# In the planner that writes the order of each engine, a hop between engines counts ten times what it did

## The chip, the cores and the metric

The kernel runs on one core of a Trainium2 chip. Five engines of that core matter here: PE (matrix multiplies), ACT (activations and copies), DVE (vector operations), POOL (here almost only the issue of gathers from memory) and SP (the issue of plain transfers). Each engine works through its own list of instructions in the order in which they are written, and they meet only through semaphores: an instruction whose data another engine makes waits for that engine's semaphore, and what stands behind it on its own engine waits as well.

The metric is the device time of one execution in microseconds. It is given as the median of three plain executions. Beside it there is one execution under the hardware profiler, which takes longer and from which all durations of single instructions come.

## What is computed

The input is 16 graphs of 1024 nodes with 64 channels, and an adjacency matrix for each graph in float32. Per graph, the reference normalizes the node features and clips them at zero, drops one or two neighbours, chosen by their rank, of every node that has more than ten (in both directions), and then takes, for every node and channel, a weighted sum of the three quartiles over the neighbours that remain and the node itself. A small two-layer perceptron follows, and the input is added:

```
h = relu(layernorm(x))
adj_d = adj without the edges dropped by rank (made symmetric)
s = sort over neighbours of h[neighbour]          # per node, per channel
agg = 0.25*q(0.25) + 0.5*q(0.5) + 0.25*q(0.75)    # quantiles read from s, interpolated
y = relu((h + agg) @ W1 + b1) @ W2 + b2
out = x + y * mask
```

## The kernel before

The fast path (`list_layer`; a dense path stands behind a flag that is not set with these inputs) goes through the 16 graphs as 8 pairs. For each graph there is a preparation and an aggregation.

The preparation of a graph is spread over PE, ACT and DVE. `load` reads the adjacency in eight tiles of 128x1024 (line 870), takes its sign on ACT (958), transposes it on PE (965) and writes it back from PSUM by ACT or DVE (978). `drop` computes the distance of each neighbour's rank from the two ranks that are dropped (PE 1035 and 1040, ACT `dist` 1045) and compares on DVE (`rem` 1046). `keep` puts the kept edges together (PE 1058 to 1063, ACT 1068) and packs them to codes (PE 1071, ACT 1076). `order` sorts the nodes by how many neighbours they have (DVE `num` 1082 onwards, `perm` 1117), and `collect` permutes the codes (PE 1142) and reads the neighbours' numbers out of them with repeated maxima on DVE (1151, 1174). The result is a list of row numbers per graph (`idx`, 1186).

The aggregation of a pair begins with gathers: POOL issues one indirect transfer per neighbour slot and tile of 128 nodes (line 1329, 952 of them, and 34 of kin for a special group of nodes with many neighbours, lines 1681, 1685 and 1749). DVE then runs sorting networks over the gathered lines (minima and maxima, lines 1434 to 1442), ACT or DVE scales the chosen lines (1457, 1459), PE adds them up (1463), and the perceptron follows (1564 to 1660).

The Python code emits all this pair by pair; it then hands the whole list of instructions to `arrange`, which decides in what order each engine executes its own. `arrange` makes a `Step` of each instruction, with an estimate of how long it occupies its engine (`busy`) and how long after that its result can be used (`lag`; 200 for PE, 150 for ACT, 80 for DVE, 950 for a gather after 1345 of issue, 1500 and more for a transfer of SP, all in planned ns). It collects the dependencies, the reuse of buffers among them, and walks over the graph of steps forward and backward: each walk is list scheduling, in which an engine that is free takes, of the steps whose inputs are ready, the one of lowest rank. The backward walk gives the ranks for the next forward walk. Six rounds are made (`ROUNDS`), the sequence with the shortest planned end is kept, and it is written down as the order of each engine with ordering edges.

`between(s, o)` is what a walk adds between the end of step `s` and the start of a dependent step `o`. If they are on different engines, or `s` is a transfer, it is the lag and a constant; on DVE itself it is 115, and on the other engines zero.

Two more things come out of the kept walk. Each gather waits until the last gather but one has been issued (`paced`). And each gather is tied to DVE by a leash: it may not be issued before the DVE step that by the plan had ended 25,000 ns (`LEASH`) ahead of it.

Of the kernel before, what the change touches and what calls it, by code (L numbers as in the profile page):

```python
# [70 lines left out]
GROUP = 8  # L71
SLICE = P // GROUP
SECOND = 14
ROUNDS, LEASH = 6, 25000


TURNED = (0, 1, 3, 2, 0, 1, 3, 2)
# [590 lines left out]

def between(s, o):

    return s.lag + 60 if o.engine != s.engine or s.moves else 115 if s.engine == "DVE" else 0


def forward(steps, ranks):

    left, ready = [len(s.before) + len(s.behind) for s in steps], [0.0] * len(steps)
    starts, sequence, wire = [0.0] * len(steps), {e: [] for e in ENGINES}, [0.0]

    def place(s, when, free_to_go):
        starts[s.place] = when  # L680
        sequence[s.engine].append(s)
        end = when + s.busy
        if s.engine == "SP":
            wire[0] = max(wire[0], end) + s.load
            s.lag = wire[0] + 1500 - end
        for o in s.after:
            ready[o.place] = max(ready[o.place], when if s.place in o.behind else end + between(s, o))
            left[o.place] -= 1
            if not left[o.place]:
                free_to_go(o.place, ready[o.place])  # L690

    total = spread(steps, list(left), ranks, place)
    return sequence, starts, total


def backward(steps, starts):

    left, ready, ends = [len(s.after) for s in steps], [0.0] * len(steps), [0.0] * len(steps)

    def place(s, when, free_to_go):  # L700
        ends[s.place] = when + s.busy
        for p in (*s.before, *s.behind):
            o = steps[p]
            ready[p] = max(ready[p], when + s.busy - o.busy if p in s.behind else when + s.busy + between(o, s))
            left[p] -= 1
            if not left[p]:
                free_to_go(p, ready[p])

    spread(steps, list(left), [-(starts[s.place] + s.busy) for s in steps], place)
    return [-t for t in ends]  # L710
# [99 lines left out]
def list_layer(  # L810
# [682 lines left out]
    def aggregate(m, o, between=None):  # L1493
# [4 lines left out]
        for half in (0, 1) if last else (1, 0):  # L1498
            parts = CLASSES[2 * half:2 * half + 2][::1 if last else -1]
            for sides in ((0, 1), (1, 2)) if last and half else ((0, 2),):  # L1500
# [13 lines left out]
                if one is not None:  # L1514
                    yield from between(one, False)
# [528 lines left out]
```

## Time and profile before

| | |
|---|---|
| median of three plain executions | 1444.05 us |
| lowest and highest of the three | 1441.54 and 1449.81 us |
| the profiled execution's own time | 1901.87 us |
| its span, first to last instruction | 1900.1 us |
| busy in the span: PE, DVE, ACT, POOL | 1228.6, 1226.8, 1069.1, 1027.3 us |
| mean granted clock of PE | 0.809 |

The profiled execution is longer than a plain one by 458 us. A share of busy time is to be read against the span of 1900.1 us of the profiled execution, not against the median. The busy time of PE is modelled and its matrix multiplies overlap, so that it overstates how full PE is. A line of the profile's page gives, for a group of like instructions, the source line, engine, operation, the tiles written and read, the count, the busy time in us with the mean in ns, and after the second bar the idle time of that engine just before them, with what ended most of it.

### The profile page before, as it was taken

What the parts mean: (1) busy time and instruction counts of PE and PEld (TensorE: products, weight loads), DVE (VectorE), ACT (ScalarE), POOL (GpSimd) and SP (SyncE); (2) the same over time, 40 slices, a digit from 0 to 9 for tenths busy, and PEclk for the clock granted to TensorE, in tenths of its full rate; (3) what the DMA queues carried; (4) which work ended last, traced back from release to release, by engine and by line L of the source; (5) the groups of instructions that cost most, each with busy time, mean ns of one, the idle gap of its engine ahead of it and who ended that gap; (6) DMA issues with size and microseconds to landing.
All of it is one profiled execution on the core that took longest, in us unless ns stands there. A gap on an engine that the chain in (4) does not pass through costs nothing. (4 is left out here: it accounts for less than half of the span.)

```text
span 1900.1 us, 30251 instructions
## 1 busy us (share of the span) xinstructions
PE 1228.6 (65%) x8995; PEld 770.5 (41%) x9011; DVE 1226.8 (65%) x5869; ACT 1069.1 (56%) x2869; POOL 1027.3 (54%) x991
## 2 busy tenths in 40 slices
PE   6637566577867587667664687655873678733847
PEld 4424344254444344344432444433542345511434
DVE  5515277653676758774658658586757745596895
ACT  7646356466663578355662657353673675323765
POOL 0354564644564646554557455465565645577780
PEclk9769689597888798878877798767986789866868
DMA  5423232212331214121322123231230110112110
GB/s 185 137 76 92 61 92 67 83 50 68 84 102 43 86 39 137 42 73 45 102 79 50 54 47 104 54 94 32 54 71 18 31 21 20 19 23 49 27 31 15
DMA packets 128832, 121.67 MB, mean 64 GB/s; under 512 B 95730, under 2 KB 96274, under 8 KB 128658
## 3 DMA queue, kind: packets, MB, share of 16 engines
q1 hardware_dynamic: 97106, 87.29, 15.3%
q0 software_dynamic: 31552, 32.36, 8.7%
q8 instruction: 73, 1.20, 0.3%
q14 instruction: 101, 0.83, 0.1%
HBM read 108.79 MB, written 9.05 MB: 62 GB/s over the span
## 5 line engine op out<-in xcount | busy, mean ns | idle before, releaser
L1329 POOL DMA_INDIRECT g<-gtab,idx x952 | 989.4, 1039 | 816.3 <-issue 211.8
L1437 DVE TENSOR_TENSOR g<-g 128x384 f32<-128x384 f32 (+2 forms) x659 | 310.9, 492 | 25.1 <-issue 10.7
L1442 DVE TENSOR_TENSOR g<-g 128x384 f32<-128x384 f32 (+2 forms) x659 | 310.1, 491 | 10.1 <-DMA gg<-g 6.0
L1142 PE MATMUL codeP<-pack,perm 128*128 128x332 bf16 x1024 | 191.7, 332 | 59.2 <-DVE perm L1117 38.3
L1045 ACT ACTIVATE dist<-rk,bias 128x512 f16<-128x512 f32 x256 | 169.2, 701 | 84.5 <-remote 44.2
L1068 ACT ACTIVATE kept<-kp 128x512 fp8e4<-128x512 f32 x224 | 133.4, 600 | 132.9 <-remote 61.1
L978 ACT ACTIVATE ne<-tp 128x512 fp8e4<-128x512 f32 x248 | 143.4, 612 | 102.7 <-remote 67.4
L965 PE MATMUL tp<-kb,sg 128*128 128x128 bf16 x1024 | 119.9, 250 | 98.7 <-issue 37.5
L1463 PE MATMUL acc<-g,kf 128*128 128x128 f32 (+2 forms) x472 | 146.2, 446 | 55.7 <-ACT g L1457 35.5
L1035 PE MATMUL rk<-kb,cnt 128*128 128x512 bf16 x256 | 113.7, 444 | 93.6 <-ACT dist L1045 47.4
L1142 PEld LDWEIGHTS <-perm 128*128 128x128 bf16 x1024 | 100.1, 105 | 151.5 <-DVE perm L1117 49.4
L1040 PEld LDWEIGHTS <-ne 128*128 128x128 fp8e4 x1024 | 91.0, 110 | 154.7 <-issue 131.1
L1046 DVE TENSOR_SCALAR rem<-dist,half 128x1024 bf16<-128x1024 f16 x128 | 62.9, 493 | 129.4 <-ACT dist L1045 120.0
L965 PEld LDWEIGHTS <-sg 128*128 128x128 bf16 x1024 | 89.2, 113 | 140.8 <-issue 119.6
L1071 PE MATMUL code<-kw,kept 128*128 128x17 fp8e5 x1024 | 66.2, 175 | 122.4 <-ACT kept L1068 74.5
L958 ACT ACTIVATE sg<-at 128x1024 bf16<-128x1024 f32 x122 | 130.6, 1070 | 4.8 <-DMA at<-in_adj_dram 4.7
L1457 ACT ACTIVATE g<-g,coef 128x64 f32<-128x64 f32 x336 | 87.8, 339 | 79.0 <-DVE g L1437 44.1
L1058 PE MATMUL kp<-ne,kw 128*128 128x512 fp8e4 x256 | 112.7, 441 | 23.0 <-ACT cnt L1007 8.4
L1071 PEld LDWEIGHTS <-kept 128*128 128x128 fp8e4 x1024 | 54.1, 102 | 175.8 <-ACT kept L1068 98.6
L856 DVE MEMSET pause<- 128x1 bf16 x2043 | 120.5, 59 | 2.3 <-issue 2.3
L1463 PEld LDWEIGHTS acc<-g,kf 128*128 128x128 f32 x472 | 87.5, 224 | 84.0 <-ACT g L1457 43.1
L1040 PE MATMUL rk<-kw,ne 128*128 128x128 fp8e5 x1024 | 120.5, 245 | 0.0
(202 smaller groups left out, 2489.2 us busy)
## 6 DMA issues: line engine op xcount, KB each, us to landing
at<-in_adj_dram SPq DMA_DIRECT2D x122, 512.0 KB
g<-gtab,idx POOLq DMA_INDIRECT x952
xt<-in_x_dram SPq DMA_DIRECT2D x16, 256.0 KB
y<-in_x_dram SPq DMA_DIRECT2D x16, 256.0 KB
gtab<-xt SPq DMA_DIRECT2D x16, 256.0 KB
out_dram<-y SPq DMA_DIRECT2D x14, 256.0 KB
spare<-in_adj_dram SPq DMA_DIRECT2D x6, 512.0 KB
gg<-g SPq DMA_DIRECT2D x32, 48.0 KB
```

Of the source, the lines that this page charges most:

```text
L856: tails[nc.vector.memset(pause[:, at:at + 1], 0.0).ins.name] = ins.ins.name
L958: nc.scalar.activation(sg, at, AF.Sign)
L965: run.append(nc.tensor.matmul(tp[:, s], sg[:, m * P:(m + 1) * P], ident16, start=(s == 0), stop=(s == 3 and t // 4 != n), skip_group_check ...
L978: nc.scalar.activation(to, tp, AF.Relu, saturate=False)
L1040: run.append(nc.tensor.matmul(rk[:, s * P:(s + 1) * P], ne[:, 4 * n + s, ts], upper, start=False, stop=(s == 3), skip_group_check=True,))
L1045: nc.scalar.activation(dist[:, n * HALF:(n + 1) * HALF], rk, AF.Abs, bias=bias[:, t:t + 1])
L1068: nc.scalar.activation(kept[:, 4 * n:4 * n + 4], kp, AF.Relu, saturate=False)
L1142: run.append(nc.tensor.matmul(flat, perm[:, t, k * P:(k + 1) * P], pack[:, t], start=False, stop=(t == NT - 1), skip_group_check=True,))
L1329: ins = nc.gpsimd.indirect_dma_start(out=gathered[m, tiles][:, slot, k - lo, h], out_offset=None, in_=tables[2 * m + h][0], in_offset=bass ...
L1437: nc.vector.tensor_tensor(at(f + k * df, df, many), pa, pb, OP.min if what == "<" else OP.max)
L1442: nc.vector.tensor_tensor(pa if back else pb, pa, pb, OP.max if what == "<" else OP.min)
L1463: nc.tensor.matmul(acc, ident32, lines[:, s], start=False, stop=(s == now[-1] and not ends), skip_group_check=True)
```

## The change

One constant is added, and the planner's hop from one engine to another (or from a transfer to its user) becomes the lag and 600 instead of the lag and 60. No instruction, tile, buffer or constant of cost is touched beside it; ranks, order, and the places at which the leash is tied follow from the walks.

```diff
-ROUNDS, LEASH = 6, 25000
+ROUNDS, LEASH, LATE = 6, 25000, 600
...
 def between(s, o):

-    return s.lag + 60 if o.engine != s.engine or s.moves else 115 if s.engine == "DVE" else 0
+    return s.lag + LATE if o.engine != s.engine or s.moves else 115 if s.engine == "DVE" else 0
```

## The prediction

> **What bounds the kernel now.** I read the page's totals first, then POOL's gathers in order of time, the waits, the end of the chain, and the busy time by stretch.
>
> From the page, totals and two groups:
>
> ```profile
> span 1900.1 us, 30251 instructions
> PE 1228.6 (65%) x8995; PEld 770.5 (41%) x9011; DVE 1226.8 (65%) x5869; ACT 1069.1 (56%) x2869; POOL 1027.3 (54%) x991
> ...
> L1329 POOL DMA_INDIRECT g<-gtab,idx x952 | 989.4, 1039 | 816.3 <-issue 211.8
> ...
> L1046 DVE TENSOR_SCALAR rem<-dist,half 128x1024 bf16<-128x1024 f16 x128 | 62.9, 493 | 129.4 <-ACT dist L1045 120.0
> ```
>
> No engine is full. POOL looks emptiest, but its shown durations are not its pace. POOL in order of time (start, duration, idle before):
>
> ```profile
> 63.14 1.10 POOL L1329 DMA_INDIRECT g<-gtab,idx  x1 [61.24 <-DVE idx L1186]
> 64.54 0.95 POOL L1329 DMA_INDIRECT g<-gtab,idx  x1 [0.30 <-issue]
> 65.80 0.94 POOL L1329 DMA_INDIRECT g<-gtab,idx  x1 [0.30 <-DMA g<-gtab,idx]
> ...
> 1676.30 1.13 POOL L1329 DMA_INDIRECT g<-gtab,idx  x1 [0.30 <-DMA g<-gtab,idx]
> 1677.73 1.13 POOL L1329 DMA_INDIRECT g<-gtab,idx  x1 [0.30 <-DMA g<-gtab,idx]
> ...
> 1854.87 0.93 POOL L1749 DMA_INDIRECT out_dram<-gx,gto  x1 [1.46 <-DMA out_dram<-gx,gto]
> ```
>
> Back to back, 0.30 us always stays between two gathers: the pace is 1.25 us when quiet and 1.43 us when busy. POOL's 991 instructions are 986 transfers and 5 small ones at the start (1.4 us busy). So POOL occupied is 1025.9 + 986 x 0.30 = 1321.7 us. The head before the first gather is 63.1 us, the tail after the last transfer 1900.1 - 1855.8 = 44.3 us. 63.1 + 1321.7 + 44.3 = 1429.1; POOL waited for the other 471.0 us of the span.
>
> The waits (us in total, times, longest):
>
> ```profile
> POOL g L1329 <- issue: 211.8, 446, 14.1
> DVE rem L1046 <- ACT dist L1045: 120.0, 43, 19.0
> DVE num L1082 <- ACT pack L1076: 88.5, 11, 17.3
> ACT st L1155 <- DVE keys L1151: 82.8, 28, 22.2
> PE code L1071 <- ACT kept L1068: 74.5, 43, 8.5
> POOL g L1329 <- DVE g L1442: 69.4, 47, 12.7
> ```
>
> PE, ACT and DVE wait in turn for each other, and POOL for DVE, mostly by the leash. By gather number POOL's waits are even: some 415 of the 471 us fall before the 800th.
>
> The plain run. The profiled execution (1901.87) is 457.8 us above the median of 1444.05, which is almost what POOL waits. If head and tail are in a plain run what they are here, 1444 - 1429 = 15 us of waiting are left there; if they shrink like the whole (factor 0.759, 107.4 to 81.5), 41 us. **So in a plain run POOL is nearly the bound: about 28 us of idle time, with DVE (1226.8 of 1444 us, 85%) close behind.**
>
> **What the skill says.** Trainium skill, "Perfetto Trace Analysis", "GPSIMD Engine Instruction": a span there is unreliable, and starts of consecutive instructions should be compared. The trace agrees: 0.95 us shown, 1.25 us apart. The same page, "Tensor Engine Instruction (MATMUL, LD_WEIGHTS)": ACT, DVE and GPSIMD are strict FIFO. The trace agrees: `rem` held DVE for up to 19.0 us. "DMA: Bandwidth & Descriptors", "Anatomy of one DMA": a fixed cost of about 2.0 us, mostly completion; the chain below has 2.47 us for a gather. The first walk counts 1345 + 950 + 60 = 2355 ns, the new one 2895.
>
> **The change, part by part.** Instructions, transfers and buffers are the same on every engine; the price of what is removed or added is nothing. Only places change.
>
> The real hop, from the chain that ended last:
>
> ```profile
> 1569.22 2.47 DMA g<-gtab,idx
> ...
> 1762.23 0.59 ACT highs L1621
> 1762.87 2.07 PE hp L1627 x2
> ```
>
> PE starts 0.05 us after ACT's recorded end. The planner's old 210 (ACT) to 260 ns (PE), counted from the engine's release, are near that; 750 to 800 are too long. The plan is thus no truer, it has more room.
>
> (1) Room between producer and user. I took both built orders, and for each wait on another engine summed the mean durations (profile's rows) of the instructions of the waiting engine that stand between the user and the last instruction of its own that must precede the awaited one. Medians, before and after: PE waiting for ACT 3.26 and 4.68 us, ACT for PE 1.90 and 2.60, DVE for PE 2.38 and 3.29, DVE for ACT 4.68 and 5.52. ACT's waits for PE with under 2 us of room fall from 575 to 356. PE's rows overlap, so only the comparison counts. The waits among PE, ACT and DVE shown above are those whose room grows.
>
> (2) POOL's demands. By order and waits together, the 300th gather needs 375 us of DVE work finished before, 313 after; the 600th 766 and 694; the 800th 1021 and 978; the 900th 1129 and 1094. For 43 to 72 us DVE may be later than now without POOL noticing, 35 to 54 gathers at 1.34 us. I count two thirds of the waits before gather 800 as gone: 415/471 x 28 = 25 us, two thirds are 16 us. From below: none, if the waits that remain in plain runs are of the late part; from above all 41.
>
> (3) Head. Ahead of the first gather stand 70 ACT instructions in place of 83 (49 us of rows for 55, ACT being 48.35 of 63 us busy there), 833 of PE for 887, 125 of DVE for 130. But SP's first two transfers become the constants (222 and 144 KB), and the adjacency tile that starts ACT comes third; in the trace ACT starts on it at 4.29 us. At the 178 GB/s of that stretch 366 KB are 2 us. Together 6 - 2 = 4 us earlier; bounds -8 and +4. By the 20th gather 82 us of ACT are needed for 74, by the 50th 107 for 109: the gain is given back there, and I count 0.
>
> (4) Tail. After the 980th gather hang 30 us of DVE for 19, 28 of ACT for 22, 48 of PE for 42. Part lies beside each other: +3 us; bounds 0 and 11. The last two fetches of `gx` (L1685) move to POOL's end, next to the scatter; two places, no new transfer. SP's other moves (28 places at most) are transfers issued tiles ahead; POOL's gather order is the same for 750 of 996 places: 0.
>
> Sum: -16 + 0 + 3 = -13 us of the plain run. On the profiled execution the waits are larger (471 us), and it should fall by more, some 50 to 120 us. Since (2) could as well be the whole 25, I take -16: **1428 us**.
>
> **The rivals.**
> - *Gathers already saturated* (chance 0.21). In favour: the 15 us end above. Then the order is not felt: 1444, within 7.
> - *Late backlog, slower* (0.20). The work taken from before the gathers is still to be done: behind gather 800, DVE has 250 us where it had 178 (1271 us in all). 186 gathers at 1.34 are 249 us, so that from there on DVE must be nearly full, in the stretch where it runs the long sorts:
>
> ```profile
> core 0: us, PE busy (x) PEld busy (x) DVE busy (x) ACT busy (x) POOL busy (x), PEclk, DMA share, GB/s
> 1600.00:1700.00 100.00, 56.50 (x431) 43.98 (x430) 68.08 (x295) 38.94 (x125) 62.01 (x59) 0.80 0.11 20
> 1700.00:1800.00 100.00, 54.84 (x251) 30.56 (x251) 72.18 (x329) 49.17 (x123) 71.94 (x62) 0.74 0.18 39
> 1800.00:1900.00 100.00, 59.20 (x292) 38.60 (x293) 75.58 (x198) 61.33 (x177) 45.04 (x31) 0.76 0.11 22
> ```
>
> Mean share 0.72. With the plain head of 48 us gather 800 is due at 48 + 800 x 1.34 = 1120; 250/0.72 = 347 gives 1467. It decides when the share is under 250/(1444 - 1120) = 0.77. Against it: this execution is stretched; scaled by 85/65 the share is 0.94, and 1120 + 266 = 1386 doesn't bind.
> - *Large gain* (0.07). If plain gathers keep the quiet pace, 986 x 1.25 = 1233, and waits in plain runs are 1444 - 1233 - 82 = 129; a third gone gives about 1400. Against: the busy stretches show 1.43.
> - *No effect on the order* (0): all five orders differ; DVE's instructions move by 30 places in the median, 754 at most.
>
> **How the numbers follow.** The forecast has 0.52. Likeliest 1428, its own range 1408 to 1438. A difference under 0.5% (7 us) is about what a measurement of this kernel can't tell from none. Nearly all of the forecast's case and the large gain lie beyond it: faster 0.58; same 0.21, slower 0.21. For 8 in 10 the range runs from 1398, so that half the large gain is left out, to 1463, so that the upper part of the backlog is.
>
> **What would show.** Right: in the new profile POOL's idle time at L1329 falls well under 816 us, `rem` waits for `dist` under 120, the head stays near 63 us, and DVE's share after 1600 us rises. Wrong: POOL's idle stays, or moves to the last 200 gathers; the tail exceeds 55 us; or sorts wait for gathers, which would say that a longer plan let POOL fall behind.

## The result, and the profile after

The changed kernel takes 1467.71 us in the median of four executions (1466.74 to 1469.96); the kernel before, in its four of the same comparison, 1445.86 us. The ratio is 1.0155, with a 95% interval of 1.0135 to 1.0175: slower by 22 us, where the forecast was 16 us faster.

The 458 us by which the profiled execution of before lies over the plain ones are not a cost of profiling, as the text ahead of the prediction has it. In e1_base, the same kernel, the profiled execution took 1443.97 us, among ten executions from 1441.34 to 1447.28. And on one other chip (the runs e9 to e12) 43 executions of before took 1895.36 to 1928.04 us, with 1901.87 us well inside. So the first profile was most likely taken on such a chip, though its chip is not on record. It can't be laid beside a profile of 1464.9 us; e1_base supplies one of before at 1442.3 us.

The page of the changed kernel, totals and gathers:

```profile
span 1464.9 us, 30188 instructions
PE 1151.5 (79%) x9011; PEld 731.7 (50%) x9011; DVE 1220.3 (83%) x5869; ACT 1047.2 (71%) x2869; POOL 1055.2 (72%) x991
...
L1329 POOL DMA_INDIRECT g<-gtab,idx x952 | 1012.3, 1063 | 357.3 <-DMA g<-gtab,idx 141.3
```

The page of the kernel before, run again (e1_base):

```profile
span 1442.3 us, 30251 instructions
PE 1103.4 (77%) x8995; PEld 709.9 (49%) x9011; DVE 1220.6 (85%) x5869; ACT 1041.3 (72%) x2869; POOL 1046.6 (73%) x991
...
L1329 POOL DMA_INDIRECT g<-gtab,idx x952 | 1005.4, 1056 | 355.3 <-DMA g<-gtab,idx 127.5
```

Of the 355.3 us of idle time before, 952 x 0.30 = 286 us are the fixed distance between gathers and 61.7 us the head; some 8 us are left. In the changed kernel it is 357.3 us, nearly the same. POOL waits for next to nothing in either. What differs is what DVE has done by the time of a given gather. Busy time by stretch, cut at the start of POOL's first, 300th and 900th transfer and at the end; transfers are counted from 0 here and below, so that 86 of the 986 lie behind the last cut. First the kernel before (e1_base):

```profile
core 0: us, PE busy (x) PEld busy (x) DVE busy (x) ACT busy (x) POOL busy (x), PEclk, DMA share, GB/s
63.30:462.90 399.60, 332.34 (x3108) 214.79 (x3109) 333.52 (x1604) 333.35 (x887) 307.50 (x301) 0.97 0.41 116
462.90:1268.60 805.70, 621.07 (x4918) 400.85 (x4926) 713.10 (x3676) 551.12 (x1602) 619.45 (x600) 0.89 0.28 72
1268.60:1442.30 173.70, 105.23 (x517) 64.92 (x521) 135.08 (x455) 108.53 (x294) 118.50 (x86) 0.78 0.15 34
```

and the changed kernel, cut at the same transfers:

```profile
64.40:458.90 394.50, 311.05 (x2675) 199.91 (x2673) 279.98 (x1326) 294.31 (x784) 300.35 (x300) 0.86 0.37 106
458.90:1272.70 813.80, 671.16 (x5247) 423.65 (x5245) 749.73 (x3883) 587.38 (x1674) 629.13 (x601) 0.91 0.29 77
1272.70:1464.90 192.20, 122.96 (x648) 77.42 (x647) 152.10 (x532) 116.71 (x325) 124.59 (x86) 0.78 0.14 31
```

The gathers run at the same pace, but during the first 300 DVE does 280.0 us of work in place of 333.5. In the next 600 it recovers 36.6 us of the 53.5, and 17.0 us more are left behind gather 900. The 22.6 us between the spans are: head 1.1, first 300 gathers -5.1, next 600 +8.1, the rest +18.5. A second profile of the changed kernel on another chip (e15_changed) repeats it: 278.5 us of DVE in the first stretch, and 152.7 in a last stretch of 196.9 us. DVE is not alone: behind gather 900 PE too has 17.7 us more (123.0 for 105.2) and ACT 8.2. DVE is the busiest of the three there, 79% of the stretch for PE's 64%.

Why DVE does less: what it waits for, the kernel before (e1_base) and then the changed one (us in total, times, longest us):

```profile
DVE rem L1046 <- ACT dist L1045: 29.9, 23, 2.8
DVE keys L1151 <- PE codeP L1142: 27.0, 40, 1.2
...
DVE g L1437 <- DMA g<-gtab,idx: 6.1, 3, 3.6
```

```profile
DVE g L1437 <- DMA g<-gtab,idx: 48.7, 16, 10.9
DVE keys L1151 <- PE codeP L1142: 33.0, 34, 2.2
DVE g L1528 <- ACT g L1525: 27.0, 6, 7.5
DVE rem L1046 <- ACT dist L1045: 26.5, 20, 3.5
```

A wait that is small in the kernel before stands first: sorts wait for gathers, 48.7 us for 6.1. The same view for the first stretch of the changed kernel alone (64.4 to 458.9 us) has among others:

```profile
DVE g L1437 <- DMA g<-gtab,idx: 24.9, 7, 10.9
...
DVE g L1528 <- ACT g L1525: 14.0, 3, 7.5
DVE var L1244 <- ACT var L1243: 9.4, 2, 5.9
```

In that stretch DVE is idle for 114.5 us in place of 66.1. Of the 48.4 us more, 24.9 are sorts that wait for gathers (none there before), 13.4 are the step at line 1528, which waits for ACT, 8.6 are `var`, and the rest lies in smaller waits, up and down. In the new order sorting steps come ahead of preparation steps: by the 100th gather DVE has done 35 sorting steps for 23 before, and 93.7 us of preparation (lines below 1230) for 109.1. In the three longest of those waits for gathers (8.4, 3.7 and 10.9 us) the next preparation step stands 4 to 9 instructions behind, and it begins without a wait when its turn comes; that its input was there during the wait is not shown. The wait that the forecast wanted to shrink, `rem` for `dist`, loses 3.4 us.

### The profile page after: what moved, and what is told of

It is laid out like the page before. It is cut to its first block, busy times and chain, and to the rows that moved or that the text cites. A ratio compares the mean times of both kernels' runs of the same rounds, so it can differ in the third digit from the quotient of the medians.

```text
span 1464.9 us, 30188 instructions
## 1 busy us (share of the span) xinstructions
PE 1151.5 (79%) x9011; PEld 731.7 (50%) x9011; DVE 1220.3 (83%) x5869; ACT 1047.2 (71%) x2869; POOL 1055.2 (72%) x991
## 5 line engine op out<-in xcount | busy, mean ns | idle before, releaser
L1329 POOL DMA_INDIRECT g<-gtab,idx x952 | 1012.3, 1063 | 357.3 <-DMA g<-gtab,idx 141.3
L1437 DVE TENSOR_TENSOR g<-g 128x256 f32<-128x256 f32 (+2 forms) x659 | 312.4, 492 | 51.2 <-DMA g<-gtab,idx 48.7
L1442 DVE TENSOR_TENSOR g<-g 128x384 f32<-128x384 f32 (+2 forms) x659 | 310.7, 492 | 3.5 <-DMA gg<-g 2.6
L965 PE MATMUL tp<-kb,sg 128*128 128x128 bf16 x1024 | 113.5, 243 | 56.7 <-ACT dist L1045 28.5
L1142 PEld LDWEIGHTS <-perm 128*128 128x128 bf16 x1024 | 97.5, 102 | 86.0 <-DVE perm L1117 22.9
L1040 PE MATMUL rk<-kw,ne 128*128 128x128 fp8e5 x1024 | 113.9, 239 | 0.0
L1063 PEld LDWEIGHTS <-rem 128*128 128x128 bf16 x1024 | 80.5, 99 | 66.8 <-issue 10.6
L1155 ACT CAST st<-codeP 128x4 bf16<-128x4 f32 x128 | 21.2, 166 | 126.9 <-DVE rest L1153 87.4
L1058 PE MATMUL kp<-ne,kw 128*128 128x512 fp8e4 x256 | 99.4, 390 | 14.6 <-ACT kept L1068 10.0
L1463 PEld LDWEIGHTS acc<-g,kf 128*128 128x128 f32 x472 | 79.5, 212 | 53.0 <-ACT g L1457 23.4
L1059 PE MATMUL kp<-rem,kw 128*128 128x512 bf16 x256 | 99.9, 390 | 2.8 <-DVE pause L856 1.5
```

The lines of the kernel that those rows point to most:

```text
L965: run.append(nc.tensor.matmul(tp[:, s], sg[:, m * P:(m + 1) * P], ident16, start=(s == 0), stop=(s == 3 and t // 4 != n), skip_group_check ...
L1040: run.append(nc.tensor.matmul(rk[:, s * P:(s + 1) * P], ne[:, 4 * n + s, ts], upper, start=False, stop=(s == 3), skip_group_check=True,))
L1142: run.append(nc.tensor.matmul(flat, perm[:, t, k * P:(k + 1) * P], pack[:, t], start=False, stop=(t == NT - 1), skip_group_check=True,))
L1329: ins = nc.gpsimd.indirect_dma_start(out=gathered[m, tiles][:, slot, k - lo, h], out_offset=None, in_=tables[2 * m + h][0], in_offset=bass ...
L1437: nc.vector.tensor_tensor(at(f + k * df, df, many), pa, pb, OP.min if what == "<" else OP.max)
L1442: nc.vector.tensor_tensor(pa if back else pb, pa, pb, OP.max if what == "<" else OP.min)
```

## The experiments

All sixteen run against the kernel before on their own chip; the ratio to that kernel, with its 95% interval, says more than the time. "Held" is the sum, over the last 86 transfers of POOL, of what each shows over 1.4 us, taken from POOL in order of time: what gathers lose by lasting long. The two theories at the start: A, that the loss lies behind gather 900; B, that the gathers' pace falls throughout.

**e1_base: the kernel before again.**

```diff
-ROUNDS, LEASH, LATE = 6, 25000, 600
+ROUNDS, LEASH, LATE = 6, 25000, 60
```

> The kernel before, with the hop of 60 written as the constant. The profile on record of before was stretched to 1900 us; this one should be near its median, 1446 us, so that the two orders can be compared gather by gather. Theory A (the late part): POOL's gathers already keep their pace through the middle here too, at 1.30 to 1.36 us each, with few waits, and the 100th to 900th gather take within 10 us of what they take in the changed kernel (1077 us); what the changed kernel loses lies in the last 86 gathers, which take 154 us there and some 130 us here, and in what is tied to them. Theory B (the whole pace): the gathers run at 1.32 us in the middle here against 1.35 us there, some 20 us over 800 gathers, and the last 86 take the same in both.

Ratio 1.0006. The 100th gather starts at 191.2 us and the 900th at 1268.6: 1077.4 us, and 1077.2 in the changed kernel. B falls. The last 86 take 145.6 us here and 153.8 there, less apart than A had it; the tail after them is 28.1 us and 38.4.

**e2_moves and e3_engines: which hops.** The longer hop for landings alone, then for hops between engines alone (in this cut and the one of e9 and e10, `...` stands for the rest of the line, and the names behind `#` are added here):

```diff
-    return s.lag + LATE if ...
+    return s.lag + (LATE if s.moves else 60) if ...      # e2_moves
+    return s.lag + (60 if s.moves else LATE) if ...      # e3_engines
```

> The change alone for the results of transfers and gathers (lag and 600), while hops between engines keep lag and 60. Theory A: what hurts is where the late gathers and the vector work that uses them are put; if the longer landing makes that, this version is as slow as the changed kernel, 1460 to 1470 us. If the hops between PE, ACT and DVE make it, it stays within 8 us of the kernel before, 1438 to 1454 us. Theory B expects it near the kernel before, since transfers are few and a busier mixture comes from the hops between engines.

> The change alone for hops between engines (lag and 600), while the results of transfers and gathers keep lag and 60. The other half of the run before it: near 1467 us if the hops between PE, ACT and DVE carry the loss, within 8 us of 1446 us if the landings do. Theory B expects 1460 to 1470 us here.

e2_moves: 1438.56 us, ratio 0.9992 (0.9963 to 1.0021). e3_engines: 1461.4 us, 1.0112 (1.0083 to 1.0142). The hops between the engines carry the loss, or most of it. In e3 DVE has 154.6 us left at gather 900, in e2 129.6.

**e4_mid: a hop of 240.**

```diff
-ROUNDS, LEASH, LATE = 6, 25000, 600
+ROUNDS, LEASH, LATE = 6, 25000, 240
```

> The hop counts 240 (four times the old one). If the loss grows with the hop as the plan's length does, some 7 us over the kernel before, 1453 us. If it comes from single places of the order, as theory A has it, the time need not lie between the two; anything from 1430 to 1475 us.

1448.16 us, 1.0023 (1.0006 to 1.004), and 136.4 us of DVE behind gather 900 (135.1 before). Between the two, nearer to the old end, and below the 1453 us of a loss that grows with the hop; the range given for single places was too wide to tell anything.

**e5_rows: the fetches of gx.** At the end of the changed kernel DVE stands for `gx`, whose fetches had moved to POOL's end:

```profile
DVE gx L1660 <- DMA gx<-in_x_dram,gto: 7.7, 1, 7.7
```

The edit, in `arrange`, holds the last pair's gathers into the tiles g6 back behind them:

```diff
+    rows = [s for s in steps if s.engine == "POOL" and any(u.tile.name.startswith("gx") for u in s.writes)][-2:]
+    for s in steps:
+        if s.engine == "POOL" and s.place > rows[-1].place and any(u.tile.name.startswith("g6") for u in s.writes):
+            s.behind.update(o.place for o in rows)
```

> The changed kernel, but the planner is told that the two fetches of gx (L1685) stand ahead of the last pair's g6 gathers on POOL; by the order of the build they then stand at places 950 and 951 of 986, as in the kernel before, and not at 982 and 983. Theory A: at the end of the changed kernel DVE waits 7.7 us for gx (L1660), with the last sorts behind it. That wait goes, the tail after POOL's last transfer falls from 38 us towards 28 to 31, and the time is 1457 to 1461 us. Rival C (the tail is bound by PE's and ACT's own work, and DVE's wait is slack): 1465 to 1469 us.

1471.0 us, 1.0189 (1.0139 to 1.0239): nothing gained. The wait for `gx` is gone, and the waits of sorts for gathers behind gather 900 go from 8.1 to 25.6 us. A's part about `gx` isn't borne out. It isn't a clean test, though, since one gather lasts 13.93 us here and the held time goes from 30.6 to 38.7 us.

**e6_paused, e7_base_paused, e8_both: held gathers.** In the changed kernel two gathers last 12.0 and 6.8 us (POOL in order of time: start, duration, idle before):

```profile
1331.02 1.17 POOL L1329 DMA_INDIRECT g<-gtab,idx  x1 [0.30 <-DVE gg L1442]
1332.50 11.97 POOL L1329 DMA_INDIRECT g<-gtab,idx  x1 [0.30 <-DVE y L1660]
1344.78 6.79 POOL L1329 DMA_INDIRECT g<-gtab,idx  x1 [0.32 <-DVE y L1660]
1351.87 0.94 POOL L1329 DMA_INDIRECT g<-gtab,idx  x1 [0.30 <-DMA g<-gtab,idx]
```

while DVE sorts without a gap, as it does in the last pair and the last group alone, where the 59 ns memset that otherwise follows each sorting step is left off:

```profile
1332.49 0.55 DVE L1442 TENSOR_TENSOR g<-g 128x384 f32<-128x384 f32 x1
1332.96 0.35 DVE L1437 TENSOR_TENSOR gg<-gg 128x192 f32<-128x192 f32 x1
1333.23 0.28 DVE L1434 TENSOR_TENSOR g<-g 128x128 f32<-128x128 f32 x1
```

The Trainium skill, "SBUF — State Buffer", "Who interferes with whom", says that a DVE instruction with two SBUF inputs contends with a GpSimd instruction that reads SBUF; it tells of one instruction, and here a gather is held over a long row of them. The same section infers that `tensor_tensor`, which the sorts are, doesn't stall the issue of transfers; these gathers, long beside rows of it, speak against that. The edit puts the memsets back (e6 in the changed kernel, e7 in the one before, e8 in the changed one with e5's edit too):

```diff
-        gap = (lambda ins: ins) if whole else opened
+        gap = opened
```

> The changed kernel, but the last pair's and the last group's sorts too have the small pause after each vector operation (312 pauses more, 59 ns each, 18 us of DVE). Theory A: single gathers of the changed kernel last 4 to 12 us where DVE sorts without a pause (32.5 us above 1.4 us per gather in all). With pauses no gather lasts over 2.5 us and the last 86 take some 120 us in place of 154; the time falls by 10 to 25 us, to 1443 to 1457. Here the plan also puts the two fetches of gx at 950 and 975, so up to 8 us of a gain may be theirs. Rival D (the long gathers are slack, DVE's work sets the end): 18 us of DVE are added and the time is 1470 to 1485 us.

> The same pauses in the kernel before, where the gathers' excess over 1.4 us is 24.4 us in all. Theory A: 1425 to 1440 us. Rival D: 1450 to 1462 us.

> The changed kernel with both: the fetches of gx at 950 and 951 and the pauses. If both effects are what they seem, the time is that of the kernel before with the pauses, within 8 us. If something else of the changed order costs as well (before gather 900 it is 4 us late), it stays some 5 us or more above it.

e6: 1453.85 us, 1.0061 (1.004 to 1.0083). e7: 1444.57 us, 0.9991 (0.9964 to 1.0019), its executions lying between 1431 and 1448. e8: 1453.51 us, 1.0085 (1.0051 to 1.012). Held time falls from 30.6 us (changed) and 22.9 (before) to 1.7 in e6 and e8 and 0.7 in e7. The stretch from gather 900 to the end, e7 and then e8:

```profile
1271.00:1430.70 159.70, 104.50 (x517) 64.83 (x521) 132.28 (x730) 103.14 (x270) 88.33 (x86) 0.79 0.16 37
```

```profile
1275.80:1454.20 178.40, 119.05 (x643) 75.32 (x647) 153.59 (x836) 115.21 (x318) 94.58 (x86) 0.82 0.15 33
```

The pauses take 14.0 us from this stretch in the kernel before (173.7 to 159.7) and 13.8 in the changed one (192.2 to 178.4, with e5's edit). The difference of 18.5 stays, as 18.7, though hardly a gather is held in either. In these two profiles, then, the held gathers are a cost of both kernels, and what remains is the work left over.

The medians say less. They agree for the changed kernel (14 us less) and not for the kernel before, whose median doesn't move: e7's expectation was met only by its three fastest executions, and its profile is one of these, 12 us under its median. e6 lies inside theory A's 1443 to 1457 us. With the pauses in both kernels the medians are 9 us apart (1453.5 in e8, 1444.6 in e7) and not 22. These 9 us are clear of the noise, as the intervals of e7 and e8 don't meet; whether the other 13 us of the loss go with held gathers or with the luck of single executions stays open. Of e8's two cases it is the second: something else of the changed order costs as well.

The profile of e6 also limits what the pauses do. Its profiled execution took 1467.13 us, 13 us over the median, and has two gathers of 5.26 and 8.99 us ahead of the 900th, among sorts with the memset. This one, in e11_moves_paused below, lasts over 42 memsets:

```profile
1806.98 20.68 POOL L1329 DMA_INDIRECT g<-gtab,idx  x1 [2.59 <-DVE gg L1442]
```

So the memset makes held gathers rarer, and doesn't exclude them.

**e9_early, e10_late, e12_zero, e11_moves_paused.** The longer hop for the first 12,000 of 16,027 steps, or for the others alone; a hop of the lag alone; and the landings' hop with the pauses:

```diff
+    return s.lag + (LATE if s.place < TURN else 60) if ...     # e9_early, TURN = 12000
+    return s.lag + (LATE if s.place >= TURN else 60) if ...    # e10_late
+ROUNDS, LEASH, LATE = 6, 25000, 0                              # e12_zero
```

> The longer hop only for steps that the program emits among the first 12,000 of 16,027 (up to about the 750th gather); the last quarter keeps lag and 60. In the build the order is that of the changed kernel up to gather 700 (845 us of DVE work needed before it, against 903 in the kernel before) and nears the old one by gather 900 (1109 us, against 1129 before and 1094 changed). Theory A', the backlog: vector work put off early is carried to the end, where DVE is full. Then DVE has some 12 us less than before behind it at gather 900, the excess behind gather 900 is about half of the changed kernel's 22 us, and the time is 1453 to 1463 us. Rival E (only the order of the last stage counts): within 6 us of 1445 us.

> The longer hop only for the last quarter of the steps. In the build, DVE's work needed before gathers 300, 700 and 900 is that of the kernel before (376, 903, 1127 us). Theory A': no backlog, so within 6 us of 1445 us. Rival E: 1460 to 1470 us.

> The opposite of the change: a hop counts the lag alone. In the build the demands before gathers 300 and 700 are 378 and 906 us, 3 us more than in the kernel before, so theory A' expects no more than 2 us less than the kernel before: 1440 to 1448 us. If shorter hops made the order fragile, as the forecast had it, it would be slower, 1450 us and more.

> The best parts together: the longer hop for landings alone, and the pauses in the last sorts. The landings alone had 158 us of DVE work left at gather 900 where the kernel before has 166. Expected 1425 to 1440 us; 1443 to 1447 us if neither part is worth anything by itself.

These four fell on the chip where the kernel before takes 1905.6 us. e9_early: ratio 1.0243 (1.0169 to 1.0316). e10_late: 0.9926 (0.9899 to 0.9952). e12_zero: 1.0107 (1.0047 to 1.0167). e11: 0.9974 (0.995 to 0.9998). The early steps carry a loss and the late ones a small gain there. The loss is larger than A' had it (its 1453 to 1463 us are ratios of 1.006 to 1.013), and one gather of e9 lasts 35.65 us; e10's gain is beyond the 6 us of A' too. e11, 0.26% under the kernel before, lies at the edge of what its parts together were to give and decides nothing. e12 is a miss that the demands of the order don't explain, for they are those of the kernel before; its 800th transfer starts at 1561 us in place of 1531, and its DVE work behind gather 900 is 145.8 us for 142.1. That it is the slower one says that 60 is not a point from which shorter is better.

**e15_changed, e13_early, e14_late, e16_late_paused: the halves on one chip with the changed kernel.** The edits are those of the change, of e9, of e10, and of e10 with the pauses.

> The changed kernel once more, so that it stands beside the next two on one chip. The run of the early and the late half of the change fell on a chip on which the kernel before takes 1906 us. If this one takes about 1444 us for the kernel before, 1460 to 1475 us for the changed one; if it is one of the slow kind, a ratio between 1.01 and 1.03, since the early half alone had 1.024 there.

> The longer hop for the first three quarters of the steps, beside the changed kernel. Theory A', the carried backlog: at least half of the changed kernel's loss, 1455 to 1470 us on a chip of 1444 us. Rival E (only the last stage's order counts): within 6 us of the kernel before.

> The longer hop for the last quarter alone. Theory A': at most 4 us over the kernel before; on the slow chip it was 0.7% under it, which would be 1434 us on a chip of 1444 us. Rival E: 1460 to 1470 us.

> The longer hop for the last quarter, with pauses in the last sorts. If the late half alone is a gain of 0.7% and the pauses keep the gathers from being held, 1425 to 1438 us on a chip of 1444 us; 1440 to 1450 us if neither carries over.

Beside 1441.98 us for the kernel before: e15_changed 1470.47 us, 1.023 (1.0179 to 1.0282); e13_early 1460.95 us in the median, in two groups, five executions from 1440.6 to 1459.2 and five, the profiled one among them, from 1462.8 to 1467.8; e14_late 1453.89 us, 1.0079 (1.0054 to 1.0104); e16_late_paused 1433.87 us, 0.9961 (0.9933 to 0.9989). The lower group of e13 by itself is at 1.0046 (1.0012 to 1.008), a loss of some 7 us, and the profile can't speak for it. From gather 900 to the end, e13_early, e14_late and e16_late_paused:

```profile
1273.00:1463.00 190.00, 116.19 (x570) 72.41 (x569) 142.67 (x482) 108.28 (x291) 132.98 (x86) 0.75 0.15 31
```

```profile
1272.30:1453.50 181.20, 108.08 (x521) 66.42 (x521) 127.92 (x415) 102.89 (x270) 128.98 (x86) 0.75 0.15 32
```

```profile
1272.60:1428.80 156.20, 107.73 (x521) 63.85 (x521) 131.74 (x726) 102.28 (x270) 90.74 (x86) 0.82 0.17 38
```

The early half leaves 142.7 us of DVE work there, 7.6 more than before. But its gathers are held for 43.8 us in all, 20.9 more than in the kernel before, most of it in one:

```profile
1348.46 35.47 POOL L1329 DMA_INDIRECT g<-gtab,idx  x1 [0.30 <-DMA g<-gtab,idx]
```

Its last stretch is 16.3 us longer than before, and the holding could carry all of that; the run doesn't show that the work put off costs by itself, and the early half with pauses was not run. The late half leaves 127.9, less than before, and still loses. Its gathers are held for 37.8 us in all, against 22.9 in the kernel before; with the pauses that goes to 0.5 us, and the kernel is the fastest of the four, under the one before. So the late half's loss was held gathers, which depends on where sorts and gathers happen to meet. Neither rival was right alone: expected were at most 4 us for the late half by the carried backlog (12 measured), and near nothing for the early half by the other (7 to 23, by group).

## Why the prediction was wrong

**The plain run.** "About 28 us of idle time" on POOL in a plain run was wrong: beyond the 0.30 us of each gather it is 10 us by POOL in order of time (e1_base), and 12.5 in the changed kernel. I took the profile's extra 458 us for the profile's own and scaled them down; they belong, as far as the record tells, to where it was taken. The premise of the rival "gathers already saturated" held, but not its conclusion that the order is then not felt.

**(1) Room.** The room was counted in the order, and the waits didn't follow it as a whole. Between e1_base and the changed kernel DVE's waits for ACT fell from 100.8 to 86.0 us and PE's for DVE from 147.0 to 121.0; ACT's for PE rose from 126.2 to 142.6 and PE's for ACT from 164.5 to 176.9. The step took room for gain.

**(2) POOL's demands.** This is the step that failed. "The 300th gather needs 375 us of DVE work finished before, 313 after" was right as a reading of the order, and the traces have nearly these amounts done by then (372.4 and 318.5 us, the head included). I called it freedom for POOL, worth 16 us. POOL had no use for it: with 10 us of waits in all it runs at its own pace of 1.25 to 1.43 us a gather in any case. The work was put off, not saved: +17.0 us behind gather 900, and a kernel 22 us slower. (The 43 us at 1.34 us are 32 gathers, not 35; nothing rests on it.)

**(3) Head.** 0 us forecast, 1.1 us measured.

**(4) Tail.** "+3 us" counted what hangs on the 980th gather. Counted from the 900th, where the order's change still shows, it is +18.5 us.

**The slower rival** had 1467 us, and the place of the loss is as it said: work moved behind the last gathers, which DVE must still do. Its price came out right by luck. It gave the changed kernel 250 us of DVE work behind gather 800 and the kernel before 178; by the prediction's own demands these are 1271 - 978 = 293 and 1271 - 1021 = 250, and the profile that it read already had 252.7 us behind gather 800. So its 250 us are those of the kernel before. Measured are 269.7 us of busy time in the 326.6 after 1138.3 us, a share of 0.83; in the kernel before (e1_base) 251.3 us in the 311.1 after 1131.2, a share of 0.81. The share hardly changes and the work does: 18.4 us more at 0.82 would be some 22 us, an estimate as large as the loss, but one that leaves no room for the 7.7 us by which the changed kernel's gathers are also held longer. I had set the rival aside by scaling the share to 0.94, again because of the stretched profile. Its decision point of 0.77 does not hold, as the kernel is slower with a share above it.

What I had not priced at all is the holding of gathers beside sorts, above all those without a pause: 14 us of the end stretch in either kernel's profile, and what makes the late half lose.

**What stays open.** How much of the 22 us is the work put off: 9 us by the medians with pauses, all of it by the two profiles. Whether it is DVE's own work, or PE's and ACT's beside it, since all three have more left behind gather 900. Why single executions of e2, e7 and e13 differ by up to 20 us or more; a meeting of gather and sort that depends on timing would do it, but that was only argued. Why PE's granted clock in the first 300 gathers is 0.86 in the changed kernel and 0.97 before, and whether this slows the preparation as well. It goes with the order: 0.84 to 0.87 in the seven profiles near 1450 us that have the hop of 600 between engines in the early steps, and 0.95 to 0.98 in the six others. Behind gather 900 it is 0.78 in both kernels, so that it doesn't make the 18.5 us there. And why e12_zero is slower.

## What to carry to other kernels

When a planner's order changes, ask of the engine that sets the pace not only how little must be finished before each of its steps, but how much is left for the others after its last ones: a looser demand early is a debt at the end. A latency that the planner overstates isn't by itself a safety margin. Here it put sorts ahead of preparation; that this is because chains with many hops then look late to the planner is argued from its rule, not tested. And before idle time in one profile is scaled to a plain run, take a second profile.

## What the runs showed of the hardware

Most gathers that POOL issues take 0.94 to 1.2 us in the profile, and single ones up to 35 us (35.47 in e13_early, 35.65 in e9_early) while DVE runs f32 operations on two SBUF operands almost back to back. With a memset of one column, 59 ns, after each of them, what the last 86 gathers show over 1.4 us is 0.5 to 1.7 us in all in e6, e7, e8 and e16; in e11 one of 20.68 us remains. The same program takes 1.32 times as long on one chip as on another (1905.6 and 1442 us, medians of before).
